# A planned TensorE order: two durations per operation, and stage times of their own for the first and last groups

## The chip, the cores and the metric

The kernel runs on one core of a Trainium2 chip. Five engines work side by side, each through its own list of instructions in a fixed order: PE (TensorE, matmuls and transposes; PEld is its weight load), DVE (VectorE), ACT (ScalarE), POOL (GpSimd) and SP (SyncE, which here only issues DMAs). An engine that reaches an instruction whose input is not there waits, and everything behind it on that engine waits too. The metric is the device time of one execution in microseconds; the kernel before has a median of 2764.06 us in 3 runs (2762.44 to 2764.56).

## The reference

Four graph layers on x (128 graphs, 128 nodes, 256 features) and adj (128 x 128 x 128, about 3% ones). Each layer is wrapped as `x = layernorm(x + layer(x, adj))`.

```python
# layer 0: attention by edge type (adj is 0 or 1 here)
e_k = leaky_relu(einsum('bid,bjd->bij', x * a_k, x)); alpha = where(adj == k+1, e_k, NEG_INF)
out = softmax(alpha) @ x
# layer 1: mean of messages
out = relu(x @ W_upd + (a.T @ (x @ W_msg)) / deg + bias)
# layer 2: three GRU steps
for i in range(3):
    aggr = einsum('bst,bsd->btd', A, h @ weight[i])
    gi, gh = aggr @ w_ih.T + b_ih, h @ w_hh.T + b_hh
    r, z = sigmoid(i_r + h_r), sigmoid(i_z + h_z); n = tanh(i_n + r * h_n)
    h = (1 - z) * n + z * h
# layer 3: additive attention
Wh = h @ W; e = leaky_relu(Wh @ a1 + (Wh @ a2).T); out = elu(softmax(where(adj > 0, e, NEG)) @ Wh)
```

## The kernel before

**Tiling.** The 128 graphs are taken in 32 groups of four (`G`, `NG`, lines 62 and 63). For each group the functions `loading`, `layer0`, `layer1`, `gru` (three times `step`) and `layer3` write down the group's operations; `weights` does so once for the weights. Nothing is issued at that time. A call such as `PE.matmul(...)` goes through `Engine.__getattr__` (line 188), which makes an `Op` with its engine, its operands, a planned duration and its dependences. This is why every instruction in the profile stands on one line, 232, the line of `issue`; groups of the profile are told apart by their tiles.

**The steps.** A GRU step works on features by nodes: `hT` holds two tiles of 128 features x 512 (four graphs of 128 nodes). `aggregate` multiplies the hidden state, split in three bf16 parts (`split`), by the adjacency matrix (`a_ne`) into `agT`. `gate` computes two 128 x 512 outputs of a gate with seven products instead of eight: products 1, 6, 7 and 4 are added one after another into one PSUM bank (`shared`), and after each of them ScalarE copies the bank's first half (`snapshot`, line 717) before the next may be added; products 2, 5 and 3 go into another bank. A step has gates q (hidden part of the candidate), t_r and t_z, two direct products (`direct`), and at the end `update`, which makes the new `hT` on VectorE. VectorE then transposes it in 32 x 32 blocks (`turned`), and two DMAs through DRAM (`way_h` out, `hn` back) finish the transpose; `split` makes the parts for the next aggregation. The `sums` that products 5, 6, 7 and 4 need are made on GpSimd from `hT` (`t_h`) and on VectorE from `agT` (`t_m`).

**The planner.** From line 921 a list scheduler puts the operations in order. It keeps for every engine a time at which it is free and a list of operations whose dependences are planned. It takes the engine that can start something first, and among that engine's operations that could start by then the one with the earliest due time (`nominal`; off TensorE an operation of a GRU step counts as due `EAGER` us earlier, and a snapshot `RUSH` us earlier). The chosen operation is issued, so the order of this loop is the order of the instructions on each engine. The planned times themselves are not in the program: the chip's engines start when their semaphores allow.

Three things set the plan. First, the durations (lines 239 to 256): one figure per operation, for which the engine is held and after which the result can be used, and then a hop: `HOP` to a step's operation, `PE_HOP` to one on TensorE, `SLACK` to any other; a DMA lands `LANDING` after its issue. Second, the due times: `paced(start, end)` spreads the operations recorded since the last call over a stretch, in units of `PERIOD` (82.744 us), the same for each group but for its number:

```python
    PERIOD = 82.744
    EAGER, RUSH = 5.34, 0.516
    L0_START, L0_END, L1_START, L1_END, L3_START, L3_END = -2.032, -1.293, -0.75, -0.05, 0.173, 0.919
```

So group g's layer 0 is due from g - 2.032 to g - 1.293 periods, its steps from g on, its layer 3 after step 2; several groups are under way at a time, and while one group's step waits for VectorE or a DMA, TensorE is given another's layer. Third, the buffers: a tile can be taken when the planner sees its last use done. VectorE and GpSimd share a port: an operation that `holds` it delays one that `waits` for it (lines 205 to 211 and 951).

The last group's layer 3 is written in two halves of two graphs, and the first group's and the last group's transposes go through TensorE (`turned_quick`, `end`) where the others go through DMAs.

Of the kernel before, what the change touches and what calls it, by code (L numbers as in the profile page):

```python
# [18 lines left out]
def kernel(  # L19
# [40 lines left out]
    P = 128  # L60
# [81 lines left out]

    FAST = ("tensor_scalar", "tensor_scalar_add", "tensor_scalar_mul")

    def m_of(view):
# [9 lines left out]
    class Op:  # L155
        def __init__(self, engine):
            self.engine, self.calls, self.took, self.landing = engine, [], 0.0, 0.0
            self.after, self.bufs, self.waiting = {}, [], 0
            self.ready, self.nominal, self.urgent = 0.0, 0.0, False
            self.waits = self.holds = False  # L160
            self.rush = 0.0

    class Engine:
# [24 lines left out]
        def __getattr__(self, name):  # L188
            def call(*args, **kw):
# [7 lines left out]
                ins = [v for v in (*rest, *named.values()) if isinstance(v, View)]  # L197
                n = 1
                for v in out + ins:
                    n = max(n, m_of(v))  # L200
                short = self is PE and BF16 in [v.buf.dtype for v in ins]
                op.took += SPLIT if short else self.cost(name, n, "accum_out" in kw)
                op.landing = LANDING if name == "dma_start" else 0.0

                tensors = [v for v in ins if m_of(v) > 4]
                if self is POOL:
                    op.waits, op.holds = True, name == "memset" or len(tensors) > 1
                elif self is DVE and name not in ("transpose", "bn_stats"):
                    op.waits = op.holds = not any(v.buf.pool is psum for v in out + tensors) and (
                        len(tensors) > 1 or (name in FAST and m_of(out[0]) > 4)  # L210
                    )
# [26 lines left out]

    LANDING = 4.2
    HOP = 0.235  # L240
    PE_HOP = 0.55
    SLACK = 0.873

    def pe_cost(op, n, sums):
        return 0.11 if op == "transpose" else 0.222 if n <= P else 0.003 + n / 599.0

    SPLIT = 0.056

    def dve_cost(op, n, sums):
        return 0.14 + n * (0.00056 if op in FAST else 0.00106)  # L250

    def act_cost(op, n, sums):
        return 0.6 if op == "dma_start" else 0.17 + n * 0.001 + (0.2 if sums else 0.0)

    def pool_cost(op, n, sums):
        return 0.2 + n * 0.00266 if op in FAST else 0.55 if op == "memset" else 1.2 if n < 64 else 0.25 + n * 0.0023

# [3 lines left out]
    POOL = Engine("POOL", nc.gpsimd, pool_cost)  # L261
    SP = Engine("SP", nc.sync, lambda op, n, sums: 0.6)
    engines = (PE, DVE, ACT, POOL, SP)


    PERIOD = 82.744
    SPAN = 2.0
    EAGER, RUSH = 5.34, 0.516
    L0_START, L0_END, L1_START, L1_END, L3_START, L3_END = -2.032, -1.293, -0.75, -0.05, 0.173, 0.919
    H_END, M_START, M_END = 0.179, 0.179, 0.503  # L270

    def paced(start, end, pe_only=False):

        took = [op.took if not pe_only or op.engine is PE else 0.0 for op in line]
        total, sofar = sum(took), 0.0
        for op, t in zip(line, took):
            op.nominal = (start + (end - start) * sofar / total) * PERIOD
            op.urgent = pe_only
            sofar += t
        line.clear()  # L280

    def row(v, n):
# [25 lines left out]
    def weights():  # L308
# [3 lines left out]
        for src, tag, bufs in ((w_ih, "hT", 6), (w_hh, "rest", 4)):  # L312
# [4 lines left out]
            if src is w_ih:  # L317
                for i in range(NL):
                    w = tile_of("hn", [P, KC, D], 3)
                    ACT.dma_start(out=w, in_=weight[i].rearrange("(c p) e -> p c e", p=P))  # L320
                    wnat.append(w)
        paced(-2.6, -2.5)
        for k, a in enumerate((a0, a1, a2, a3)):
            SP.dma_start(out=acol[:, k, :], in_=a.rearrange("(c p) -> p c", p=P))
        paced(-2.2, -2.1)
        SP.dma_start(out=w_um[:, :, :D], in_=w_upd.rearrange("(c p) u -> p c u", p=P))
# [6 lines left out]
        SP.dma_start(out=arow, in_=row(a_att, 2 * D))  # L333
        paced(-2.0, -1.5)

# [81 lines left out]
        for c in range(KC):  # L417
            DVE.tensor_sub(w3x[:, c, :], w3x[:, c, :], ps[:, : 2 + D])
        paced(-1.9, -0.2)

# [87 lines left out]
    def loading(g, s):  # L508
        graphs = slice(g * G, (g + 1) * G)
        s.x_blocks = tile_of("x_blocks", [P, KC, 4 * G, 32])  # L510
        s.adj = tile_of("adj_in", [P, G, N], 1, I32)
        s.x = tile_of("x_in", [P, G, D])
        for c in range(KC):
            for j in range(4):
                f0 = c * P + j * 32
                SP.dma_start(
                    out=s.x_blocks[j * 32 : (j + 1) * 32, c],
                    in_=x[graphs, :, f0 : f0 + 32].rearrange("b (i r) f -> r (b i) f", r=32),
                )
        SP.dma_start(out=s.adj, in_=adj[graphs].rearrange("b i j -> i b j"))  # L520
        paced(g - 2.4, g - 2.1)
        SP.dma_start(out=s.x, in_=x[graphs].rearrange("b n d -> n b d"))
        paced(g - 1.9, g - 1.8)

# [118 lines left out]
    def gru(g, s):  # L643
# [5 lines left out]
        def step(i, hT, parts):  # L649
# [53 lines left out]
            def gate(tag, q, sources, copied, added, last=None):  # L703
# [14 lines left out]
                def snapshot(quarter):  # L718
                    copied(t[:, quarter], shared[:, :H], quarter // 2)
                    ops[-1].rush = RUSH  # L720

# [59 lines left out]

            at = g + i * SPAN / NL
            w_i = c_gi[:, i]
            of_h = sums(POOL, hT, w_hhT, w_sh, hT, "t_h")
            q0, q1 = gate("q", C, (of_h,), hidden, half_more)
            paced(at, at + H_END, True)
            aggregate(0)
            aggregate(1)
            paced(at + M_START - 0.03, at + M_START, True)
            of_m = sums(DVE, agT, w_i, w_sm[:, i], agps, "t_m")  # L790
# [5 lines left out]
            update(0, z0, n0, d0)  # L796
            paced(at + M_START, at + M_END, True)
            return new, turning, split_up
# [104 lines left out]
    for g in range(NG):  # L903
        s = State()
        loading(g, s)
        layer0(g, s)
        paced(g + L0_START, g + L0_END)
        layer1(g, s)
        paced(g + L1_START, g + L1_END)
        gru(g, s)  # L910
        if g < NG - 1:
            layer3(g, s, 0, G)
            paced(g + SPAN + L3_START, g + SPAN + L3_END)
        else:

            for b in range(0, G, 2):
                layer3(g, s, b, b + 2)
                paced(g + SPAN + L3_START, g + SPAN + L3_END)

# [28 lines left out]
    def start_of(op):  # L948

        at = op.ready  # L950
        if op.waits:
            at = max(at, (POOL if op.engine is DVE else DVE).held)
# [18 lines left out]
    while left:  # L971
        best = None
        for e in engines:
# [5 lines left out]
            if best is None or at < best[0]:  # L979
                op = min(  # L980
                    (op for t, op in starts if t <= at),
                    key=lambda op: op.nominal - (EAGER if op.urgent and e is not PE else 0.0) - op.rush,
                )
# [7 lines left out]
        e.ready.remove(op)  # L991
        e.free = at + op.took
        if op.holds:
            e.held = e.free - 0.14
        end = e.free + op.landing
        for buf in op.bufs:
            buf.left -= 1
            buf.free_at = max(buf.free_at, end)
        for other in op.after.values():
            other.waiting -= 1  # L1000
            hop = 0.0 if other.engine is e and not op.landing else SLACK if not other.urgent else HOP
            if hop == HOP and other.engine is PE:
                hop = PE_HOP
            other.ready = max(other.ready, end + hop)
            if other.waiting == 0:
# [30 lines left out]
```

## Time and profile before

| what | us |
| --- | --- |
| median of 3 runs | 2764.06 (2762.44 to 2764.56) |
| profiled execution, first to last instruction | 2761.8 |
| PE busy | 2702.3 (98%) |
| DVE busy | 2304.1 (83%) |
| POOL, ACT busy | 1666.2 (60%), 1584.2 (57%) |
| DMA engines | 117 GB/s on average |
| mean granted TensorE clock | 0.991 |

The profiled execution's own time beside its span is not given separately: its span of 2761.8 us lies 2.3 us under the median. "Busy" of PE needs care: a matmul's record lasts 0.16 us beyond the moment at which the next may start, so an idle time under 0.16 us is not seen as idle, and a shown one is 0.16 short. The clock is the share of full speed that was granted to TensorE. In the timeline, records of one kind that follow each other are merged ("x2"), and the bracket tells idle time and who ended it. An fp32 matmul makes two records.

### The profile page before, as it was taken

The numbers are of one execution on the slowest core, as the hardware profiler recorded it, in microseconds if no ns is written. First come the engines' busy times: TensorE is split into PE (matmuls) and PEld (weight loads), VectorE is DVE, ScalarE is ACT, GpSimd is POOL, SyncE is SP. The second block draws the span as 40 slices with busy tenths as digits, with TensorE's granted clock in tenths as the row PEclk, the third lists the DMA queues.
The fourth block names the chain that finished last, engine by engine and source line by source line (L and its number), as shares of the span: only waits on it lengthen the run. The fifth ranks groups of instructions, "written<-read, shape, count | busy, mean of one in ns | idle before, by whom it ended". The sixth has DMA issues, their size and how long they took to land.

```text
span 2761.8 us, 44048 instructions
## 1 busy us (share of the span) xinstructions
PE 2702.3 (98%) x13756; PEld 2138.1 (77%) x13756; DVE 2304.1 (83%) x5108; ACT 1584.2 (57%) x3704; POOL 1666.2 (60%) x1606
## 2 busy tenths in 40 slices
PE   8899999999999999999999999999999999999996
PEld 5677787887887887887887887887887887787774
DVE  5787888888888888888888888888888898888875
ACT  4454665555665655665655665655665655665554
POOL 4544666655666655666655666655676655675542
PEclk9999999999999999999999999999999999999996
DMA  5545555555555556555655556655556555545441
GB/s 121 129 90 99 115 126 129 120 109 124 122 125 131 121 108 129 118 124 133 121 107 127 121 121 134 121 110 123 121 121 134 124 109 120 116 110 118 99 88 43
DMA packets 1397130, 321.88 MB, mean 117 GB/s; under 512 B 1142560, under 2 KB 1388448, under 8 KB 1396896
## 3 DMA queue, kind: packets, MB, share of 16 engines
q1 hardware_dynamic: 1394448, 316.69, 53.7%
q10 hardware_dynamic: 2448, 2.36, 0.3%
q8 instruction: 111, 1.82, 0.3%
q14 instruction: 123, 1.01, 0.1%
HBM read 185.74 MB, written 133.15 MB: 115 GB/s over the span
## 4 chain that ended last, share of the span: by engine, by line
PE 94%; DVE 3%; POOL 1%; ACT 1%; DMA 1%; issue 1%; ACTq 0%; POOLq 0%; DVEq 0%; SPq 0%
PE gate L232 52%; PE ps L232 42%; DVE t_r L232 0%; POOL t_h L232 0%; DVE xb L232 0%; DVE st L232 0%; DMA rest<-in_L_gnn_w_hh_dram 0%; DVE z L232 0%; POOL rstd L232 0%; DMA hn<-in_L_gnn_weight_dram 0%; POOL xa L232 0%; DVE xa L232 0%; DVE t_d L232 0%; POOL t_d L232 0%; DVE hT L232 0%
## 5 line engine op out<-in xcount | busy, mean ns | idle before, releaser
L232 ACT ACTIVATE q<-gate,bhn 128x256 f32<-128x256 f32 x384 | 183.0, 477 | 314.4 <-PE gate L232 313.1
L232 PE MATMUL ps<-agT,c_gi 128*128 128x512 f32 x768 | 356.0, 592 | 0.0
L232 PE MATMUL gate<-t_h,w_hhT 128*128 128x256 f32 x1152 | 345.2, 381 | 5.7 <-ACT t_z L232 4.3
L232 PE MATMUL gate<-t_h,w_sh 128*128 128x256 f32 x1152 | 337.1, 383 | 4.2 <-ACT q L232 1.7
L232 POOL TENSOR_TENSOR rstd<-rstd,neg_half 128x4 f32<-128x4 f32 (+1 forms) x128 | 142.4, 1112 | 218.2 <-DVE rstd L232 215.1
L232 PEld LDWEIGHTS gate<-t_h,w_sh 128*128 128x128 f32 x1152 | 213.7, 191 | 62.8 <-issue 30.4
L232 PEld LDWEIGHTS ps<-xs,xT 128*128 128x128 f32 x2048 | 249.7, 193 | 11.5 <-ACT xs L232 2.6
L232 PEld LDWEIGHTS gate<-t_h,w_hhT 128*128 128x128 f32 x1152 | 211.7, 191 | 56.1 <-issue 16.3
L232 PE MATMUL ps<-xs,xT 128*128 128x128 f32 x2048 | 251.8, 276 | 2.2 <-ACT xs L232 1.3
L232 ACT COPY t_z<-gate 128x256 f32<-128x256 f32 x288 | 107.1, 372 | 244.6 <-PE gate L232 244.0
L232 PE MATMUL ps<-w_um,x1T 128*128 128x512 f32 x512 | 237.1, 595 | 0.2 <-ACT x1T L232 0.2
L232 PEld LDWEIGHTS ps<-agT,c_gi 128*128 128x128 f32 x768 | 145.8, 190 | 114.5 <-issue 106.0
L232 PE MATMUL gate<-agT,c_gi 128*128 128x256 f32 x768 | 229.2, 380 | 2.6 <-ACT agT L232 2.6
L232 PE MATMUL gate<-t_m,c_gi 128*128 128x256 f32 x768 | 228.5, 379 | 0.0
L232 PE MATMUL gate<-t_m,w_sm 128*128 128x256 f32 x768 | 228.4, 379 | 0.0
L232 PE MATMUL gate<-hT,w_hhT 128*128 128x256 f32 x768 | 222.8, 385 | 5.6 <-DVE hT L232 5.6
L232 POOL TENSOR_SCALAR mk<-a_f 128x512 uint8<-128x512 f32 x128 | 201.3, 1579 | 12.2 <-DVE alpha L232 6.6
L232 ACT ACTIVATE xs<-xT,acol 128x512 f32<-128x512 f32 x256 | 182.1, 717 | 40.9 <-PE ps L232 31.5
L232 POOL MEMSET hu<- 128x1 f32 x128 | 10.3, 96 | 303.8 <-DVE fac L232 224.5
L232 DVE TENSOR_TENSOR t_z<-gate,t_z 128x256 f32<-128x256 f32 x192 | 104.2, 543 | 101.4 <-ACT t_z L232 53.7
L232 POOL TENSOR_TENSOR t_d<-h0T,t_n 128x512 f32<-128x512 f32 x64 | 82.9, 1295 | 174.0 <-ACT t_n L232 171.1
L232 PEld LDWEIGHTS gate<-hT,w_hhT 128*128 128x128 f32 x768 | 141.8, 191 | 48.1 <-issue 23.6
(197 smaller groups left out, 7280.1 us busy)
## 6 DMA issues: line engine op xcount, KB each, us to landing
way_h<-z SPq DMA_DIRECT2D x190, 256.0 KB, 2.4
hn<-way_h SPq DMA_DIRECT2D x760, 64.0 KB, 2.4
way<-z SPq DMA_DIRECT2D x126, 256.0 KB, 3.2
x_blocks<-in_x_dram SPq DMA_DIRECT2D x256, 64.0 KB, 2.3
x_in<-in_x_dram SPq DMA_DIRECT2D x32, 512.0 KB, 3.8
way_x<-xb SPq DMA_DIRECT2D x32, 512.0 KB, 2.9
way_p<-z SPq DMA_DIRECT2D x62, 256.0 KB, 2.6
probT<-way_p SPq DMA_DIRECT2D x248, 64.0 KB, 2.3
```

What stands on the lines that cost most here:

```text
L232: getattr(self.engine, name)(*[a.real() if isinstance(a, View) else a for a in args], **{k: a.real() if isinstance(a, View) else a for k, ...
```

## The change

The planner's model and its due times are replaced; the operations, their dependences and the buffers stay as they are.

- An operation has two durations: `took`, for which its engine is held, and `lasts`, after which its result can be used. Each engine's cost function returns both and sees the operands: operands in PSUM, pointers (small per-partition operands), type.
- DMA landing times are given by tile (`LANDING`), 2.4 us where none is named, plus `DMA_SLACK` for what follows.
- The hops are 0.1223 us (`HOP`), 0.0904 (`PE_HOP`, to TensorE) and 0.3008 (`SLACK`); none from TensorE to TensorE.
- An operation of GpSimd or VectorE minds the shared port only if it holds the port itself; `waits` is gone.
- `PERIOD` is 82.17434. Due times are in us, by stage (`TIMES`; each GRU step has its own), with an offset per stage for each of the first six groups (`HEAD`) and the last six (`TAIL`). `RUSH` becomes a factor.

```diff
-    LANDING = 4.2
-    HOP = 0.235
-    PE_HOP = 0.55
-    SLACK = 0.873
-
-    def pe_cost(op, n, sums):
-        return 0.11 if op == "transpose" else 0.222 if n <= P else 0.003 + n / 599.0
...
-    def dve_cost(op, n, sums):
-        return 0.14 + n * (0.00056 if op in FAST else 0.00106)
-
-    def act_cost(op, n, sums):
-        return 0.6 if op == "dma_start" else 0.17 + n * 0.001 + (0.2 if sums else 0.0)
...
+    LANDING = {"e": 5.66, "adj_in": 4.0, "x_in": 3.85, "x1T": 3.53, "way_1": 3.2, "way_2": 3.0, "xc": 3.6, "way_f": 2.0}
...
+    def pe_cost(op, n, out, ins, pointers, sums):
+        split = any(v.buf.dtype == BF16 or v.steps[-2:-1] == (("bitcast", (BF16,), {}),) for v in ins)
+        took = 0.11 if op == "transpose" else 0.056 if split else 0.005 + m_of(out[0]) / 600.0
+        return took, took + 0.165
+
+    def dve_cost(op, n, out, ins, pointers, sums):
...
+        elif op in FAST + ("tensor_copy", "memset") and not in_psum(out + ins):
+            lasts = 0.145 + n * 0.00055
+        else:
+            lasts = 0.145 + n * 0.00106 + (0.07 if pointers else 0.0)
+        return lasts - 0.08 + (0.05 if sums else 0.0), lasts + (0.1 if sums else 0.0)
+
+    def act_cost(op, n, out, ins, pointers, sums):
+        if op == "dma_start":
+            return 0.6, 5.0
+        lasts = 0.162 + n * 0.00083 + 0.1 * pointers
+        return lasts - 0.104 + (0.12 if sums else 0.0), lasts + (0.11 if sums else 0.0)
...
+    def sp_cost(op, n, out, ins, pointers, sums):
+        return 0.55, LANDING.get(tag_of(out[0]) if out else "out", 2.4)
...
-    PERIOD = 82.744
-    SPAN = 2.0
-    EAGER, RUSH = 5.34, 0.516
-    L0_START, L0_END, L1_START, L1_END, L3_START, L3_END = -2.032, -1.293, -0.75, -0.05, 0.173, 0.919
-    H_END, M_START, M_END = 0.179, 0.179, 0.503
+    PERIOD = 82.17434
+    EAGER, RUSH = 6.3715, 0.5988
+    HOP, PE_HOP, SLACK, DMA_SLACK = 0.1223, 0.0904, 0.3008, 1.3968
+    STAGES = ("loading", "layer0", "layer1", "step0", "step1", "step2", "layer3")
+    TIMES = {
+        "loading": ((-192.0355, -194.8256), (-195.1940, -218.9603),),
+        "layer0": ((-184.2411, -119.2739),),
...
+    HEAD = (
+        (15.258, -41.724, -22.713, -15.756, -24.319, -11.692, -19.589),
...
+    TAIL = (
+        (9.621, -0.848, 16.081, -0.054, 9.477, -4.187, 4.687),
...
+    def paced(stage, part, g):
+
+        start, end = TIMES[stage][part]
+        at = g * PERIOD
+        if g < len(HEAD):
+            at += HEAD[g][STAGES.index(stage)]
+        elif g >= NG - len(TAIL):
+            at += TAIL[g - NG][STAGES.index(stage)]
+        spread(at + start, at + end, stage[:4] == "step")
...
     def start_of(op):
 
         at = op.ready
-        if op.waits:
+        if op.holds:
             at = max(at, (POOL if op.engine is DVE else DVE).held)
...
         e.free = at + op.took
+        end = at + op.lasts + (DMA_SLACK if op.dma else 0.0)
         if op.holds:
-            e.held = e.free - 0.14
-        end = e.free + op.landing
+            e.held = at + op.lasts - 0.12
...
-            hop = 0.0 if other.engine is e and not op.landing else SLACK if not other.urgent else HOP
-            if hop == HOP and other.engine is PE:
-                hop = PE_HOP
-            other.ready = max(other.ready, end + hop)
+            to_pe = other.engine is PE
+            if e is PE and to_pe:
+                ready = e.free
+            elif e is other.engine and not op.dma:
+                ready = end
+            else:
+                ready = end + (SLACK if not other.urgent else PE_HOP if to_pe else HOP)
+            other.ready = max(other.ready, ready)
```

Since the loading stage's second time lies before its first and each stretch runs from its later to its earlier end, a group's load of x_in is now due ahead of its x_blocks, and the blocks are due in reverse order.

## The prediction

> **What bounds the kernel now.** I read the busy times first, then one table of stages, then TensorE's waits and its timeline where the table shows idle time.
>
> ```profile
> span 2761.8 us, 44048 instructions
> PE 2702.3 (98%) x13756; PEld 2138.1 (77%) x13756; DVE 2304.1 (83%) x5108; ACT 1584.2 (57%) x3704; POOL 1666.2 (60%) x1606
> ```
>
> The table: stage, its length, busy us of PE, PEld, DVE, ACT, POOL, then granted clock.
>
> ```profile
> 0.00:83.00 83.00, 67.54 (x362) 49.90 (x362) 51.63 (x130) 35.78 (x77) 43.59 (x54) 0.98 0.58 128
> 83.00:165.00 82.00, 76.84 (x368) 57.86 (x369) 53.48 (x118) 38.36 (x88) 33.33 (x36) 0.98 0.51 104
> 1000.00:1083.00 83.00, 83.00 (x428) 66.19 (x427) 71.60 (x159) 49.08 (x116) 52.73 (x51) 1.00 0.58 122
> 2482.00:2565.00 83.00, 80.63 (x376) 62.15 (x375) 69.41 (x151) 43.57 (x101) 46.45 (x45) 0.98 0.51 107
> 2648.00:2731.00 83.00, 70.90 (x300) 52.03 (x299) 53.12 (x108) 38.34 (x93) 27.37 (x27) 0.90 0.31 67
> 2731.00:2762.00 31.00, 11.13 (x31) 6.62 (x29) 15.18 (x49) 16.94 (x44) 8.35 (x9) 0.59 0.13 43
> ```
>
> TensorE is the bound, and in the interior it is full. The chain of waits there repeats one piece every 82.67 us:
>
> ```profile
> 1010.79 3.44 PE ps L232 x12
> 1093.46 3.44 PE ps L232 x12
> ```
>
> From one matmul's start to the next the trace has medians of 0.216 us (256 columns), 0.429 (512), 0.112 (128 fp32), 0.218 (258), 0.056 (bf16). One group's matmuls at these come to 82.40, so a period loses 0.27 us, in pieces under 0.06. All 13756 records come to 2661 us; the span has 100 more: 36 before 331 us, 7 in the interior, 57 after 2480. The change can gain only at the two ends.
>
> Timeline of TensorE at three idle places (start, length, what, idle time before it and who ended it):
>
> ```profile
> 109.11 0.60 PE L232 MATMUL ps<-hu,a_f 128*128 128x257 f32 x2
> 112.11 1.22 PE L232 MATMUL gate<-hT,w_hhT 128*128 128x256 f32 x2 [2.40 <-DVE hT L232]
> 113.12 2.94 PE L232 MATMUL ps<-x_in,probT 128*128 128x256 f32 x8
> 115.89 0.59 PE L232 MATMUL gate<-t_h,w_hhT 128*128 128x256 f32 x2
> ...
> 2516.80 0.70 PE L232 MATMUL gate<-agT,c_gi 128*128 128x256 f32 x2 [1.72 <-ACT agT L232]
> ...
> 2717.61 0.59 PE L232 MATMUL gate<-t_m,w_sm 128*128 128x256 f32 x2
> 2718.67 0.70 PE L232 MATMUL gate<-t_h,w_sh 128*128 128x256 f32 x2 [0.46 <-ACT t_z L232]
> 2719.21 0.59 PE L232 MATMUL gate<-t_m,w_sm 128*128 128x256 f32 x2
> 2724.76 0.63 PE L232 MATMUL ps<-ident,hT 128*128 128x128 f32 x4 [1.86 <-DVE hT L232]
> ```
>
> An idle time is dearer than it looks. The pair at 2717.61 would hand over after 0.43; the next starts after 1.06 and its pair takes 0.54: 0.46 idle costs 0.73. After 2.40 idle the next ten records run at half speed (eight take 2.77 instead of 1.73).
>
> The rule for this is in the Trainium skill, "TensorE: Matmul & The Clock Gate", section on the HAM clock gate: the clock halves after an idle window of about 3.4 us. The rows show it halved after 2.40 already (granted clock 0.60 from 112 to 116); by the page's figure that stall would be worth 2.6 rather than 4.2, and the head's sum below 1.6 less.
>
> **The change, part by part.** No instruction is added or removed; the planner puts the same 15746 operations in another order. I built both and compared orders.
>
> *Durations.* The planner's figures now are the rows: the copy 128x256 that takes 0.372 was planned as 0.426 plus 0.55 before TensorE may use it, now as 0.374 plus 0.09. In itself this costs nothing on the chip; it shows in the order.
>
> *Close pairs.* A matmul into the shared bank must wait until ScalarE has copied the bank: 0.16 (drain) + 0.04 + 0.37 + 0.05 = 0.62 us of TensorE work must stand between. Pairs closer than 0.62 number 25 in the old order and 18 in the new. In the steps of groups 0 and 1: 5 against 0. From group 28 on: 15 against 11.
>
> *Head.* (a) Between steps 0 and 1 of group 0 the old order puts layer 1 of group 1 ahead of the last z products on TensorE and VectorE; new, the update of hT comes first and layer 1 fills the wait: 4.7 us of matmuls between the last z product and the matmul that waits, where the trace needs 3.9 (108.24 to 112.11). The stall at 112.11 goes: 2.56 + 0.58 + 1.04 = 4.2. (b) Then q, rest and agT waits up to 128 us, 3.8 by the same reckoning; two of the close pairs go and rest is split earlier: 2.5. (c) Two z pairs (168, 280 us): 1.5; one agT (79 us): 0.5. Sum 8.7; ends 4 and 10.
>
> *Start.* x_in and adj of group 0 now stand ahead of all x_blocks in SP's queue, 768 KB more; at the 217 to 339 GB/s of those first 12 us this is 2.3 to 3.5 us later x_blocks, and the first scores stand behind 5.7 us of weight matmuls instead of 10.8. TensorE waits there, and the moved weight matmuls fill the softmax wait of 2.0 at 38 us. GpSimd's masks, which waited 13.8 us for adj, come sooner; TensorE did not wait for them. I take +0.6, ends -2 and +4.
>
> *Tail.* The agT stall at 2516.80 (1.88, then slowed records 1.5: 3.4), one q stall (1.0) and one z pair each in steps 2 of groups 30 and 31 (1.5) go; one z pair comes (-0.7). Two matmul pairs of group 30's layer 3 move from ahead of group 31's last z products to behind them: its hT comes 1.7 sooner. Sum 6.9; ends 3 and 8.
>
> *End.* Group 30's two output pairs (1.73) move ahead of the transposes that wait 1.86 for hT: -1.7. The transposes of wh for the last two graphs move from behind the other half's output, at 2744.57, to just behind its alpha transposes, at 2741.08 to 2741.7; the last chain hangs on them: -2.7. Together 4.4; ends 1 and 7 (the 2.66 wait at 2735 too).
>
> *Interior.* The order now has period two, with one 0.86 spacing (0.24 over the need) in odd groups and four or five in even ones; the old one has one per group, which cost nothing visible. A copy kept waiting behind one ScalarE activation of 0.72 would lose 0.48: 1.7 more such spacings a group, 28 groups, at most 23 us; at best all 7 lost now come back. I take +2: nearest to the row that shows no cost.
>
> *The other queues.* VectorE (83%), ScalarE and GpSimd carry the same work with slack; if VectorE came late by an instruction (0.69), the matmul behind it would. GpSimd's one-tensor operations no longer wait in the plan for VectorE's held port; no row prices that alone, it lies in the interior's ends.
>
> *Sum.* Gains 8.7 + 6.9 + 4.4 = 20.0. Where a stall goes, the next dependence is nearer; I let a quarter return: +5. With +0.6 and +2, 2761.8 - 12.4 = 2749.4. The median of the runs stands 2.3 above the profiled execution: 2752.
>
> **The rivals.** Measured against no change, 0.2% is 5.5 us.
>
> *Slower: the interior stalls.* Plans with 0.1 us of margin meet real jitter every period, with no idle time to absorb it. For it: TensorE at 83.00 of 83. Against: the new figures equal the rows. At the bound, 23 instead of 2: 2773. It beats the gains from 0.5 us per period.
>
> *Gains return.* Group 31's own chain (steps, then layer 3) sets the end whatever comes before, and the start's loads cost 4: only a third of 20 is left, 2752 + 9 = 2761. For it: 31 us with 11 of matmul at the end.
>
> *More.* No return, the loads hidden: 2761.8 - 20 - 2 + 2.3 = 2742.
>
> *No change at all* is excluded: the orders differ on every engine.
>
> **How the numbers follow.** Forecast 0.62, interior 0.16, return 0.14, more 0.08. The forecast's own range is 2744 to 2758. The range from 2740 to 2768 leaves out the dear end of the interior case and little below. Faster: nearly all of forecast and more, 0.68; same: most of return and the cheap part of interior, 0.16; slower: 0.16.
>
> **What would show it.** In the trace after: no wait for hT over 1 us near 110; no z wait at 168 and 280; PE busy over 80 of the second stage's 82; interior period 82.67 or less over two groups; the last alpha wait under 3.9. The prediction is wrong if the interior's period is 83.2 or more, if TensorE waits for x_blocks beyond 4 us, or if the last stage keeps its 31 us.

## The result and the profile after

The changed kernel takes 2783.71 us (median of 4 runs, 2780.87 to 2784.09), the kernel before 2764.31 in the same comparison: a ratio of 1.0068, with a 95% interval of 1.0055 to 1.0080. It is slower by 19 us where 12 us of gain were forecast, and outside the range.

The page of the changed kernel's profiled execution (span, then busy time and share of each engine):

```profile
span 2782.2 us, 43897 instructions
PE 2714.9 (98%) x13756; PEld 2129.4 (77%) x13756; DVE 2239.4 (80%) x5108; ACT 1581.6 (57%) x3704; POOL 1672.0 (60%) x1606
```

The same operations run, and VectorE is even busy for less time (2239.4 us, 2304.1 before). TensorE's records number the same, so the 20.4 us of longer span are time in which TensorE does not run at its own spacing. The stages, as the prediction showed them (stage, length, busy us of PE, PEld, DVE, ACT, POOL, clock, DMA share, GB/s):

```profile
0.00:83.00 83.00, 69.83 (x375) 52.07 (x376) 49.22 (x132) 36.58 (x79) 43.19 (x53) 1.00 0.52 128
83.00:165.00 82.00, 79.31 (x382) 61.42 (x381) 56.55 (x124) 38.64 (x87) 38.78 (x42) 0.96 0.48 99
1000.00:1083.00 83.00, 81.16 (x418) 64.11 (x418) 68.67 (x153) 47.89 (x113) 52.18 (x51) 1.00 0.57 119
2482.00:2565.00 83.00, 81.49 (x411) 63.79 (x410) 64.28 (x149) 44.08 (x103) 48.70 (x50) 1.00 0.52 106
2648.00:2731.00 83.00, 76.24 (x367) 58.03 (x365) 61.55 (x120) 43.83 (x101) 40.26 (x37) 0.95 0.44 92
2731.00:2782.00 51.00, 31.36 (x120) 21.57 (x117) 29.16 (x81) 28.30 (x74) 12.65 (x12) 0.77 0.14 37
```

The two head stages are fuller by 2.3 and 2.5 us. The stage in the interior, where TensorE was busy for 83.00 of 83, is down to 81.16 (418 records instead of 428). From here on I use one measure, the *loss*: the length of a stretch less all TensorE records that start in it, each at the median spacing that the prediction gives for its form. Both kernels have 2661.2 us of such work.

| loss, us | to 331 us (head) | 331 to 2480 (interior) | from 2480 (tail) |
|---|---|---|---|
| before | 36.1 | 7.0 | 57.5 |
| after | 29.2 | 47.2 | 44.6 |
| difference | -6.9 | +40.2 | -12.9 |

The sum is +20.4, the difference of the spans. The two ends together gained what was forecast; the interior lost twice that. TensorE's waits in the interior (who waits, for what: us in total, times, longest). The kernel after:

```profile
PE gate L228 <- POOL t_h L228: 6.8, 20, 1.6
PE gate L228 <- ACT t_z L228: 5.1, 9, 0.6
PE gate L228 <- DVE q L228: 4.9, 8, 0.7
PE gate L228 <- ACT t_r L228: 2.8, 6, 0.8
PE ps L228 <- DMA x1T<-way: 1.1, 2, 0.7
PE gate L228 <- DVE t_r L228: 0.2, 1, 0.2
```

The kernel before has the heading of this view and nothing under it:

```profile
core 0 of [0], span 2761.8 us
engine line waited for: us in total, times, longest us
```

Three engines are late in turn, none of them always. Two of these waits, followed back in the timeline of the kernel after. First one for t_h:

```profile
1254.11 0.73 POOL L228 TENSOR_TENSOR t_h<-hT 128x256 f32<-128x256 f32 x1
...
1254.68 0.71 DVE L228 SCALAR_TENSOR_TENSOR t_d<-t_z,t_d 128x512 f32<-128x512 f32 x1
...
1254.83 2.70 POOL L228 TENSOR_SCALAR xa<-xa,mv,rstd 128x256 f32<-128x256 f32 x1
1255.31 0.68 DVE L228 SCALAR_TENSOR_TENSOR xb<-xb,xa 128x512 f32<-128x512 f32 x1
1255.92 0.68 DVE L228 SCALAR_TENSOR_TENSOR hT<-t_d,t_n 128x512 f32<-128x512 f32 x1
...
1257.49 0.73 POOL L228 TENSOR_TENSOR t_h<-hT 128x256 f32<-128x256 f32 x1
...
1258.96 0.70 PE L228 MATMUL gate<-t_h,w_sh 128*128 128x256 f32 x2 [0.17 <-POOL t_h L228]
```

GpSimd's xa took 2.70 us; alone it takes 1.22. It started 0.15 us after VectorE's first two-tensor instruction, and two more followed without a gap, until 1256.60: xa got on only then. The t_h behind it came 1.5 us late; the matmul that needs it started 0.33 us late, so the rest of the delay was room. Now one in which VectorE waits for GpSimd:

```profile
1278.34 0.74 DVE L228 TENSOR_TENSOR rest<-rest 128x512 bf16<-128x512 f32 x1
...
1278.54 1.63 POOL L228 TENSOR_TENSOR t_d<-hT,t_n 128x512 f32<-128x512 f32 x1 [0.31 <-ACT t_n L228]
...
1278.97 1.22 DVE L228 SCALAR_TENSOR_TENSOR nmr<-mv,rstd 128x4 f32<-128x4 f32 x1
...
1280.22 1.09 ACT L228 ACTIVATE xb<-xb,nmr,rstd 128x256 f32<-128x256 f32 x2 [1.51 <-DVE nmr L228]
...
1281.84 0.35 ACT L228 COPY t_z<-gate 128x256 f32<-128x256 f32 x1
...
1282.23 0.70 PE L228 MATMUL gate<-t_h,w_hhT 128*128 128x256 f32 x2 [0.62 <-ACT t_z L228]
```

nmr has 4 elements a partition and takes 0.15 us alone; here it stood 1.22 us behind GpSimd's two-tensor t_d, which itself had stood behind VectorE's rest. ScalarE's two xb waited 1.51 us for nmr, the copy of t_z stood behind them and xs in ScalarE's queue, and TensorE lost 0.78 us (0.62 shown as idle, and the 0.16 by which a shown idle time is short). The same wait of TensorE comes at 1113.17 and 1452.04: 169.1 and 169.8 us apart, two groups of 84.5 to 84.9 us instead of 82.67.

The Trainium skill, "SBUF — State Buffer", section "Who interferes with whom", has the rule: VectorE and GpSimd share one pair of ports, a VectorE instruction with two SBUF inputs contends with a GpSimd instruction that reads SBUF, and the one that comes second stands still until the first is through. The rows agree for xa and nmr.

A piece of loss is the delay of one TensorE record behind its median spacing. In the whole interior 59 pieces exceed 0.15 us, 31.8 us in sum. Followed back as above over at most 6 us, some 43 of them (22 us) have an instruction on their path that was stretched by at least 60% of what was lost. Some of these can stand there by chance: the same count in e13 below, with as many stretched instructions a group, gives 15 of 59 (4.6 of 42.9 us). The kernel before has no piece over 0.06.

Yet collisions are no novelty. Counting VectorE's and GpSimd's instructions that lasted over 0.1 us more than the shortest twentieth of their kind, the kernel before has 20.0 a group, 9.2 us of stretch, and the kernel after 20.5 and 9.4. One kind in the view of groups (count, busy us, mean ns, idle before), before and then after:

```profile
L232 POOL TENSOR_SCALAR xb<-xb,mv,rstd 128x256 f32<-128x256 f32 x62 | 108.6, 1757 | 3.2
...
L232 POOL TENSOR_SCALAR xa<-xa,mv,rstd 128x256 f32<-128x256 f32 x62 | 87.9, 1420 | 3.4
```

```profile
L228 POOL TENSOR_SCALAR xa<-xa,mv,rstd 128x256 f32<-128x256 f32 x62 | 95.9, 1549 | 3.1
...
L228 POOL TENSOR_SCALAR xb<-xb,mv,rstd 128x256 f32<-128x256 f32 x62 | 78.2, 1265 | 2.3
```

Before, one of a group's two xb took some 2.47 us in nearly every group of the interior (mean 1757), and TensorE lost nothing by it; after, xb is almost free of it (1265), xa is worse, and TensorE waits. So the question for the runs was which part of the change turned harmless collisions into harmful ones.

### The profile page after: what moved, and what is told of

Read it like the earlier page. It is cut to its first block, busy times and chain, and to the rows that moved or that the text cites. A ratio compares the mean times of both kernels' runs of the same rounds, so it can differ in the third digit from the quotient of the medians.

```text
span 2782.2 us, 43897 instructions
## 1 busy us (share of the span) xinstructions
PE 2714.9 (98%) x13756; PEld 2129.4 (77%) x13756; DVE 2239.4 (80%) x5108; ACT 1581.6 (57%) x3704; POOL 1672.0 (60%) x1606
## 4 chain that ended last, share of the span: by engine, by line
PE 71%; DVE 16%; POOL 5%; ACT 3%; DMA 3%; issue 2%; SPq 1%; DVEq 0%; POOLq 0%; ACTq 0%
PE gate L228 39%; PE ps L228 31%; DVE rest L228 2%; DVE t_r L228 2%; DVE st L228 1%; DVE t_m L228 1%; DVE t_d L228 1%; POOL xa L228 1%; DVE hT L228 1%; POOL t_h L228 1%; DVE z L228 1%; SPq L228 1%; DVE xb L228 1%; POOL rstd L228 1%; POOL xb L228 1%
## 5 line engine op out<-in xcount | busy, mean ns | idle before, releaser
L228 PE MATMUL gate<-t_h,w_sh 128*128 128x256 f32 x1152 | 344.3, 385 | 9.9 <-POOL t_h L228 4.3
L228 PEld LDWEIGHTS gate<-t_h,w_sh 128*128 128x128 f32 x1152 | 207.7, 190 | 62.6 <-POOL t_h L228 15.0
L228 POOL TENSOR_TENSOR rstd<-rstd,neg_half 128x4 f32<-128x4 f32 (+1 forms) x128 | 149.3, 1166 | 163.1 <-DVE rstd L228 144.6
L228 POOL TENSOR_TENSOR t_d<-hT,t_n 128x512 f32<-128x512 f32 x128 | 177.7, 1393 | 99.5 <-ACT t_n L228 99.1
L228 POOL TENSOR_TENSOR t_d<-h0T,t_n 128x512 f32<-128x512 f32 x64 | 90.4, 1412 | 235.1 <-ACT t_n L228 235.1
L228 POOL TENSOR_SCALAR mk<-a_f 128x512 uint8<-128x512 f32 x128 | 209.6, 1643 | 22.6 <-DVE alpha L228 14.1
L228 ACT ACTIVATE t_r<-t_r,brz 128x256 f32<-128x256 f32 x192 | 117.9, 614 | 161.8 <-DVE t_r L228 150.0
L228 ACT COPY t_r<-gate 128x256 f32<-128x256 f32 x288 | 107.2, 372 | 145.5 <-PE gate L228 144.4
```

What stands on the lines that cost most here:

```text
L228: getattr(self.engine, name)(*[a.real() if isinstance(a, View) else a for a in args], **{k: a.real() if isinstance(a, View) else a for k, ...
```

## The experiments

All figures of loss are head / interior / tail, in us, as in the table above (after: 29.2 / 47.2 / 44.6); the 47.5 in the expectations is the same interior, cut a little later. Ratios are against the kernel before.

**e1, the three old margins.** The stalls look like thin margins; this puts the wide ones back.

```diff
-    HOP, PE_HOP, SLACK, DMA_SLACK = 0.1223, 0.0904, 0.3008, 1.3968
+    HOP, PE_HOP, SLACK, DMA_SLACK = 0.235, 0.55, 0.873, 1.3968
```

> The changed kernel with the three margins of the kernel before (HOP 0.235, PE_HOP 0.55, SLACK 0.873); durations, stage times, HEAD and TAIL as changed. In its order the round trips TensorE to another engine to TensorE that have under 0.3 us to spare fall from 3.7 a period to 0.7 (1.0 in the kernel before). Theory M (thin margins): the loss of TensorE from 331 to 2480 us, 47.5 us in the changed kernel and 6.9 before, falls under 15, and the time under 2765; the head and tail gains of 20 may shrink, since they were planned with the small margins. Theory W (GpSimd and VectorE planned onto their shared port at once) and theory P (a PERIOD without room): the loss stays at 35 to 50, the time at 2775 to 2790. Theory C (any reshuffle moves the time by this much): anything between 2745 and 2800.

2819.73 us, ratio 1.0201 (1.0184 to 1.0218); loss 33.3 / 61.3 / 61.7. Theory M's forecast fails: with 0.7 thin round trips a period instead of 3.7 the interior is worse, not better. (The run mixes wide margins with stage times that were set for narrow ones; e13 comes back to this.) The first wait of its interior:

```profile
PE gate L228 <- POOL t_h L228: 23.5, 33, 2.1
```

What is late most is GpSimd's t_h, by up to 2.1 us, beyond any margin of this size. The tail went back to 61.7, so the tail's gain does not outlast the small margins.

**e2, the port waits back.** In the kernel before, every GpSimd operation waits in the plan for VectorE's held port; in the change only those that hold it themselves.

```diff
-            self.holds = False
+            self.waits = self.holds = False
...
-                    op.holds = name == "memset" or len(tensors) > 1
+                    op.waits, op.holds = True, name == "memset" or len(tensors) > 1
...
-                    op.holds = not any(v.buf.pool is psum for v in out + tensors) and (
+                    op.waits = op.holds = not any(v.buf.pool is psum for v in out + tensors) and (
...
-        if op.holds:
+        if op.waits:
             at = max(at, (POOL if op.engine is DVE else DVE).held)
```

> The changed kernel in which GpSimd's one-tensor operations wait again in the plan for VectorE's held port, as in the kernel before. Theory W: the loss from 331 to 2480 us falls under 20, and the time to 2745 to 2758. Theories M and P: it stays at 35 to 55 (round trips with under 0.3 us to spare are 4.0 a period, not fewer), time 2775 to 2790.

2763.35 us, ratio 0.9997 (0.9988 to 1.0006); loss 28.7 / 25.0 / 46.5. The interior recovers 22 of its 40 us. Theory W has the direction, but both its figures (a loss under 20, 2758 us at most) are missed; the ends stay within 2 us. TensorE's waits in the interior are now

```profile
PE gate L228 <- ACT t_z L228: 3.1, 6, 0.9
PE gate L228 <- DVE q L228: 2.2, 3, 1.2
PE ps L228 <- DVE xd L228: 1.6, 1, 1.6
PE ps L228 <- PE gate L228: 0.4, 1, 0.4
```

and t_h is gone from them. Of the 25.0 us only 10.0 are left in pieces over 0.15 us (16 of them), and 5 of these (2.9 us) have a stretched instruction on their path. Collisions as a whole did not become fewer: 28.0 a group with 12.7 us of stretch, against 20.5 and 9.4. But those of GpSimd's one-tensor instructions, which the dropped rule is about, did: 1.3 us of stretch a group against 2.0. So the run does not tell whether the plan now foresees these collisions or avoids them.

**e3, the old PERIOD.**

```diff
-    PERIOD = 82.17434
+    PERIOD = 82.744
```

> The changed kernel with PERIOD 82.744 instead of 82.174, the value before; all else as changed. Theory P: the loss from 331 to 2480 us falls under 20, time 2745 to 2758. Theories M and W: it stays at 35 to 55 (3.4 thin round trips a period), time 2775 to 2790; a list order does not hold work back for a later date.

2774.99 us, ratio 1.0036 (1.0023 to 1.0049); loss 31.1 / 31.5 / 49.3. Between the theories: 16 us of the interior come back, neither under 20 nor over 35.

**e4, a change without meaning.**

```diff
-    EAGER, RUSH = 6.3715, 0.5988
+    EAGER, RUSH = 6.45, 0.5988
```

> The changed kernel with EAGER 6.45 instead of 6.3715, a change without meaning that only reshuffles the order. Theories M, W and P: the loss stays within 10 us of 47.5 and the time within 8 of 2784. Theory C (the time hangs on the accident of the order): a difference of more than 10 us either way.

2778.15 us, ratio 1.0049 (1.0034 to 1.0064); loss 29.2 / 41.5 / 45.7. A mere reshuffle is worth 6 us in the interior. Smaller effects of a parameter cannot be told from it, and e3's not by much.

**e5, the kernel before without the port waits.**

```diff
-                    op.waits, op.holds = True, name == "memset" or len(tensors) > 1
+                    op.waits = op.holds = name == "memset" or len(tensors) > 1
```

> The kernel before with one part of the change alone: GpSimd's one-tensor operations no longer wait in the plan for VectorE's held port. Theory W (the dropped port wait makes collisions that the plan does not see, and t_h comes late from GpSimd): the loss of TensorE from 331 to 2480 us rises from 7 to 20 to 35, with waits for t_h, time 2778 to 2795. Theory T (the tables of the first and last six groups and the new stage times do it; the waits only matter with them): the loss stays under 14, time 2758 to 2771.

2763.57 us, ratio 0.9997 (0.9987 to 1.0006); loss 35.2 / 11.8 / 53.5. Alone the dropped waits cost the interior 5 us, which the ends gave back. Theory W as I had put it ("20 to 35") is wrong for this order; the figures are those of theory T.

**e6, port waits back and no tables.** The lines of e2, and

```diff
     HEAD = (
-        (15.258, -41.724, -22.713, -15.756, -24.319, -11.692, -19.589),
...
+        (0,) * 7,
...
     TAIL = (
-        (9.621, -0.848, 16.081, -0.054, 9.477, -4.187, 4.687),
...
+        (0,) * 7,
...
```

> The changed kernel with the port waits restored and HEAD and TAIL set to zero; the new durations, margins, PERIOD and TIMES stay. Theories W and T together (the waits cost 22, the tables' offsets, which pull the groups out of one rhythm, most of the other 18): the loss from 331 to 2480 us falls to 5 to 12; the head loses the table's gain (29 back to 30 to 37), the tail keeps the margins' gain (44 to 50): time 2744 to 2757. If thin margins in themselves cost the other 18, the loss stays at 20 to 27 and the time at 2762 to 2772.

2763.37 us, ratio 0.9996 (0.9986 to 1.0006); loss 41.1 / 14.4 / 42.8. The interior is nearly calm (just over the 12 expected) and its waits amount to

```profile
PE ps L228 <- DMA x1T<-way: 0.4, 1, 0.4
PE ps L228 <- PE gate L228: 0.2, 1, 0.2
```

although collisions are at their highest, 30.8 a group with 14.1 us of stretch. Without HEAD the head is worse than in the kernel before, 41.1 where I expected 30 to 37, and that keeps the time above the 2757 expected; without TAIL the tail is as good as ever.

**e7, no tables, waits dropped as in the change.** The tables' edit of e6 alone.

```diff
     HEAD = (
-        (15.258, -41.724, -22.713, -15.756, -24.319, -11.692, -19.589),
...
+        (0,) * 7,
...
     TAIL = (
-        (9.621, -0.848, 16.081, -0.054, 9.477, -4.187, 4.687),
...
+        (0,) * 7,
...
```

> The changed kernel with HEAD and TAIL set to zero, port waits dropped as in the change. Theory W: the collisions are still unplanned, loss from 331 to 2480 us 25 to 40, time 2766 to 2782. Theory T: the loss falls under 15, time 2745 to 2760.

2799.48 us, ratio 1.0126 (1.0111 to 1.0141); loss 43.5 / 44.6 / 49.3. The interior stays bad without the tables, so they are not its cause (theory T falls); it is also worse than theory W's 25 to 40, and the time is above all expectations because the head is lost as well. The waits make 30 us between e7 and e6.

**e8, GpSimd's normalisation shortened.** The changed order, but GpSimd's share of xa, xb, xc and xd works on 32 of its 256 columns.

```diff
             for name, args, kw in op.calls:
+                if self is POOL and name in FAST and len(args) > 1 and args[0].buf is args[1].buf:
+                    args = (args[0][:, :32], args[1][:, :32], *args[2:])
                 getattr(self.engine, name)(
```

> The changed kernel's order to the last instruction, but GpSimd's normalisation (xa, xb, xc, xd; eight a group, 1.2 us each and up to 2.7 where they collide) works on 32 of its 256 columns; the other columns stay unnormalised. Theory W (these are what collides and what t_h stands behind on GpSimd): the waits for t_h (6.8 us) go, the loss from 331 to 2480 us falls from 47 to under 25, time under 2762. If the loss comes from hops or durations planned too short on ScalarE and VectorE, it stays over 38 and the time over 2774.

2785.79 us, ratio 1.0078 (1.0063 to 1.0093); loss 27.7 / 50.4 / 42.7. The wait for t_h goes as expected, the loss does not:

```profile
PE gate L230 <- DVE q L230: 14.3, 10, 1.9
...
PE gate L230 <- POOL t_h L230: 1.3, 2, 1.0
```

VectorE's q came late instead, and at least 28 of this kernel's 59 pieces over 0.15 us still have a stretched instruction on their path. So these operations alone are not the cause. My reading is that the shorter work moved GpSimd's other, two-tensor instructions onto VectorE's, and that moving one collision makes others; but the figures are also those that the expectation gave to the rival, hops or durations on ScalarE and VectorE planned too short (over 38, over 2774), and this run does not exclude it.

**e9, VectorE's small operations wait too.** As e6, and

```diff
+                    op.waits = op.waits or (name in FAST or len(ins) > 1) and not in_psum(out + ins)
```

> As e6 (port waits restored, HEAD and TAIL zero), and VectorE's small operations (rstd, nmr, ninv, 4 elements each), which neither kernel plans for the port, wait in the plan for GpSimd's lock as well. Theory U (what costs TensorE is not a collision but one that the plan has not foreseen): the instructions stretched by over 0.1 us stay near e6's 31 a period, or more than the 20 of the kernel before, and still the loss from 331 to 2480 us falls from e6's 14 to 10 or less; time 2755 to 2761. Rival (the 7 left over the kernel before come from the small margins): it stays at 12 to 17, time 2761 to 2767.

2767.87 us, ratio 1.0013 (1.0004 to 1.0022); loss 43.7 / 17.6 / 43.9. The small operations were stretched less often (1.4 a group, 3.9 in e6), but nothing was gained. Theory U, that foreseeing more collisions must calm the interior further, is not borne out for these.

**e10, e9 with HEAD.** The lines of e2 and e9, and of the tables only TAIL at zero.

```diff
     TAIL = (
-        (9.621, -0.848, 16.081, -0.054, 9.477, -4.187, 4.687),
...
+        (0.000, -0.000, 0.000, -0.000, 0.000, -0.000, 0.000),
...
```

> As e9, with the HEAD table of the change back (TAIL stays zero). Theories U and T: the head's loss returns to 28 to 30 (41 without the table), the tail keeps 42 to 44, the table's offsets cost the interior 5 to 11 over e9: time 2747 to 2757. Rival (the gains at the ends do not add up with a calm interior, because what is not lost in one place is lost in the next): time 2759 to 2766.

2753.94 us, ratio 0.9966 (0.9954 to 0.9978): faster than both kernels. Loss 26.8 / 17.8 / 45.3: the time is as the theories have it, the head gains more than expected, and HEAD's offsets cost the interior nothing over e9. The rival, that the gains do not add up, falls. Its page:

```profile
span 2751.1 us, 43992 instructions
...
PE 2705.5 (98%) x13756; PEld 2132.9 (78%) x13756; DVE 2301.1 (84%) x5108; ACT 1583.7 (58%) x3704; POOL 1688.0 (61%) x1606
```

VectorE is busy for 62 us more than in the slower changed kernel: its busy time holds the time by which its instructions are stretched, and this kernel, with more of it, is the faster one.

**e11, e10 with another PERIOD.**

```diff
-    PERIOD = 82.17434
-    EAGER, RUSH = 6.3715, 0.5988
+    PERIOD = 82.5
+    EAGER, RUSH = 6.3715, 0.516
```

> As e10, with PERIOD 82.5 (82.174) and RUSH 0.516 (0.5988). With HEAD, a PERIOD nearer to what a group really takes (82.67 in the kernel before) costs nothing in a plan whose collisions are foreseen, as it gave 16 us of the interior's loss in e3 where they were not: loss from 331 to 2480 us at or under e10's, time 2745 to 2755. If PERIOD helped in e3 by the accident of another order only: within 5 us of e10 either way.

2765.99 us, ratio 1.0003 (0.9994 to 1.0012); loss 29.0 / 30.6 / 43.8. Neither expectation holds: here a longer PERIOD (with another RUSH) costs 13 us of the interior where in e3 it gave 16. PERIOD has no direction of its own, and 13 us is what such a turn of two parameters can do by itself.

**e12, the durations and margins alone.** The changed kernel with the lines of e2, and pacing as in the kernel before.

```diff
-    PERIOD = 82.17434
-    EAGER, RUSH = 6.3715, 0.5988
+    PERIOD = 82.744
+    SPAN = 2.0
+    EAGER, RUSH = 5.34, 0.516
...
-            paced(f"step{i}", 0, g)
+            paced(at, at + H_END, True)
...
```

> The two durations and the new margins alone: stage times, PERIOD, EAGER and RUSH of the kernel before, port waits kept. Theory D (the durations and margins make the interior sensitive): its loss from 331 to 2480 us is over 15. Theory S (the stage times do): under 12, with the tail's gain in part, time 2745 to 2760. Theory J (stage times are set for one set of durations and are calm only with it): over 25, time over 2770, and e13 likewise.

2839.95 us, ratio 1.0273 (1.0257 to 1.0289); loss 41.1 / 79.7 / 56.5.

```profile
PE gate L228 <- ACT q L228: 13.8, 22, 0.7
```

The loss is far over theory S's 12; theories D and J both allow it. The largest wait in sum is now one for ScalarE's q.

**e13, the stage times alone.** The kernel before with the change's pacing.

```diff
-    PERIOD = 82.744
-    SPAN = 2.0
-    EAGER, RUSH = 5.34, 0.516
+    PERIOD = 82.17434
+    EAGER, RUSH = 6.3715, 0.5988
...
-            paced(at, at + H_END, True)
+            paced(f"step{i}", 0, g)
...
```

> The new stage times alone (PERIOD, EAGER, RUSH, TIMES, HEAD, TAIL), with the old single durations, margins and port waits. Theory D: loss from 331 to 2480 us under 12, time 2750 to 2765. Theory S: 15 to 40. Theory J: over 25, time over 2770.

2812.70 us, ratio 1.0177 (1.0163 to 1.0191); loss 34.4 / 54.2 / 61.7. Theory J: either half of the change alone is far worse than both kernels. That fits stage times that are set for one set of durations. Its losses are mostly of another kind: only 15 of its 59 pieces over 0.15 us have a stretched instruction on their path. This is also why e1, which mixed old margins with new stage times, could not tell whether margins are thin.

**e14, e10 without the small waits.** The lines of e2, and TAIL at zero; against e10:

```diff
-                    op.waits = op.waits or (name in FAST or len(ins) > 1) and not in_psum(out + ins)
```

> The changed kernel with the port waits restored and TAIL zero, HEAD as changed; the small operations wait for nothing in the plan. If HEAD with a zero TAIL makes e10 fast, this comes within 4 of e10's 2754; e9 against e6 (17.4 against 14.2 lost) says that the small waits gave nothing, so 2750 to 2757. If the small waits are what HEAD needs, 2758 to 2766.

2757.04 us, ratio 0.9975 (0.9965 to 0.9984); loss 29.6 / 21.5 / 44.2. HEAD with a zero TAIL and the old port waits carry e10; the 3 us between them are no more than a reshuffle.

**e15, e14 without the port waits.** Against the changed kernel, one edit:

```diff
     TAIL = (
-        (9.621, -0.848, 16.081, -0.054, 9.477, -4.187, 4.687),
...
+        (0.000, -0.000, 0.000, -0.000, 0.000, -0.000, 0.000),
...
```

> The changed kernel with TAIL zero, its port waits dropped as in the change: e14 without the waits. Theory W (the waits are worth 20 to 30 us in the interior whatever the rest): the loss from 331 to 2480 us is 40 to 52 where e14 has 21.7, time 2775 to 2788. Chance: within 12 us of e14 either way, so 10 to 34.

2782.73 us, ratio 1.0067 (1.0052 to 1.0082); loss 28.1 / 44.7 / 49.0. As theory W has it, and outside what chance was given. A third pair: the waits are worth 23 us of the interior.

**e16, e3 with the port waits.** The lines of e2, and

```diff
-    PERIOD = 82.17434
+    PERIOD = 82.744
```

> e3 (PERIOD 82.744) with the port waits restored. Theory W: the loss from 331 to 2480 us falls from e3's 31.7 to 5 to 18, time 2748 to 2762. Chance: within 12 us of e3 either way, so 20 to 44, time 2763 to 2787.

2763.19 us, ratio 0.9997 (0.9987 to 1.0006); loss 29.0 / 25.3 / 47.5. Only 6 us, within chance; theory W's 5 to 18 fails here. The five pairs in one table:

| interior's loss | waits dropped | waits kept | difference |
|---|---|---|---|
| change as it is (after, e2) | 47.2 | 25.0 | 22 |
| no tables (e7, e6) | 44.6 | 14.4 | 30 |
| TAIL zero (e15, e14) | 44.7 | 21.5 | 23 |
| PERIOD 82.744 (e3, e16) | 31.5 | 25.3 | 6 |
| the kernel before (e5, before) | 11.8 | 7.0 | 5 |

With the change's PERIOD the waits are worth 22 to 30 us three times out of three, more than the 6 and 13 that turns of other parameters moved. With 82.744 they are worth 5 or 6. Why the longer PERIOD bears the dropped waits isn't settled: no run separates it from the accident of the order.

Nor is it settled how the waits help. In the first three pairs the stretch of GpSimd's one-tensor instructions falls with them by 0.8, 1.1 and 0.9 us a group, or 20, 28 and 22 us over the 26 groups of the interior, close to the loss that goes; so they may help by avoiding these collisions rather than by foreseeing them. Against it, the fourth pair's falls by 1.3 us a group, 33 us, and only 6 us of loss go.

## Why the prediction was wrong

*Head, -8.7 and +0.6.* The sum is about right, -6.9 measured, but its parts are not, and that is luck. (a) The wait for hT near 110 us is gone, as TensorE's timeline after shows:

```profile
109.22 0.59 PE L228 MATMUL gate<-t_h,w_hhT 128*128 128x256 f32 x2
109.66 0.59 PE L228 MATMUL gate<-hT,w_sh 128*128 128x256 f32 x2
110.09 1.95 PE L228 MATMUL ps<-xs,xT 128*128 128x128 f32 x16
111.87 0.22 PE L228 MATMUL ps<-a_ne,hn 128*128 128x128 bf16 x1
113.24 0.23 PE L228 MATMUL ps<-a_ne,rest 128*128 128x128 bf16 x1 [1.15 <-DVE rest L228]
114.20 0.23 PE L228 MATMUL ps<-a_ne,rest 128*128 128x128 bf16 x1 [0.73 <-DVE rest L228]
```

Other matmuls run at 109 to 112; what is late next is rest, with 1.15, 0.73 and 0.48 us up to 116.24, and the granted clock is 0.57 from 114 to 122 us. So (a) and (b), 6.7 us of forecast gain between 83 and 165 us, brought 1.3 (loss 8.3 before, 7.0 after), and the second stage came to 79.31 busy us instead of the 80 I had named. (c) No z wait is left between 160 and 300 us; 165 to 331 us gained 2.9. The start was priced at +0.6 and gained: the first 83 us lost 24.2 before and 21.4 after, TensorE is busy for 2.3 us more in them and waits for x_blocks nowhere.

What I had not seen is where the gain comes from: HEAD. Without it the head loses 41.1 (e6) or 43.5 (e7), with it 29.6 (e14) or 28.1 (e15).

*Tail and end, -6.9 and -4.4.* Right: 11.3 forecast, 12.9 measured. The last wait for alpha is 1.40, under the 3.9 named; the longest of the end is now one for xT, 3.67 us, which was 2.23 before:

```profile
2750.25 0.66 PE L228 MATMUL ps<-ident,hT 128*128 128x128 f32 x4
...
2763.39 0.86 PE L228 MATMUL ps<-ident,xT 128*128 128x128 f32 x2 [3.67 <-ACT xT L228]
...
2769.18 0.77 PE L228 MATMUL ps<-ident,alpha 128*128 128x128 f32 x2 [1.40 <-ACT alpha L228]
```

From the first transposes of the last hT to the end it is 37.0 us before (from 2724.76 in the prediction's rows) and 32.0 after. The gain doesn't come from TAIL: with the waits, TAIL zero is 2.3 us better (e14 against e2), without them 4.4 worse (e15). It needs the new margins, durations and stage times together, as far as the runs go: the tail loses 56.5 to 61.7 where one of them is old (e1, e12, e13).

*A quarter of the gains returned, +5.* Not seen in the sum: 6.9 + 12.9 = 19.8, and 20.0 - 0.6 were forecast before the return. Between 83 and 165 us most of the gain did return (5.4 of 6.7); gains elsewhere that were not forecast made up for it.

*Interior, +2, ends -7 and +23.* Wrong, and this decides the result: +40.2. The prediction looked for new stalls in one place, the spacing of two uses of the shared bank around ScalarE's copy, and priced 1.7 of those a group. Such stalls exist (t_z and t_r in the view of waits), but in the one followed back above the copy is late because of what went before on VectorE. The step that failed is the one on the other queues: that GpSimd's one-tensor operations no longer wait in the plan for VectorE's port "lies in the interior's ends", as "no row prices that alone". A row did. In the profile before, one and the same operation on 128x256 had means of 1757 ns as xb and 1420 as xa; alone it takes 1.22 us. With one mk and the cast a_f that makes four stretched one-tensor instructions of GpSimd a group, 2.3 us, in that trace. Were the plan not to foresee them and TensorE to wait for each, 26 groups of the interior would pay 60 us: that is the end that the range lacked, and it holds the 40 measured. It is an upper end and no forecast: in the old order the same step cost 5 us (e5).

What the runs showed in its place: the port waits are worth 22 of the 40 us (e2), and two more pairs with the change's PERIOD have 30 and 23. The cause of the remaining 18 stays open. 10 of them are pieces over 0.15 us, most without a stretched instruction on their path, and 8 are smaller ones. With the tables at zero as well they are down to 7 (e6), but HEAD's offsets cost 7 us in one order (e14 against e6) and nothing in another (e10 against e9), and mere turns of a parameter moved 6 and 13. The half that keeps the old stage times (e12) and the half that keeps the old durations (e13) both lose more. That the new durations equal the rows, which the rival's case counted against itself, says nothing on it: they are the durations without a collision.

*The rival "the interior stalls"* had the right place, the right falsifier (a period of 83.2 or more; it is 84.5 to 84.9) and half the price, and it got a chance of 0.16. Its mechanism, 0.1 us of margin against jitter, wasn't shown: the stalls I followed back come from stretches of 0.3 to 1.5 us, and those that return do so nearly unchanged (nmr, ahead of the waits at 1113, 1282 and 1452 us, by 1.08, 1.07 and 1.07), which is no jitter, and wider margins without matching stage times made it worse (e1).

## What to carry to other kernels

When a planner drops a rule on a shared resource, look in the old profile for the same operation with different means: the excess per period, times the periods, is the upper end of the price if the plan no longer foresees it (here 60 us, of which one order paid 5 and another 22). Where the bound engine is full in every period, price an interior by that end rather than by the row that shows no cost, because one late result in 80 us is multiplied by the number of periods while the gains at the ends come once. Stage times and durations of such a planner are one set; each is tested with the other, and a meaningless turn of a parameter (here 6 us, and 13 for two parameters) tells how much of a result is accident.

## What the runs showed of the hardware

What the instruction in front is decides too, not only which comes first. The figures are medians over VectorE's two-tensor 128x512 instructions without PSUM that started while one of GpSimd had over 0.3 us to go. Behind a two-tensor instruction of GpSimd they took 0.91 us longer with 1.01 to go (108 cases of t_d in e6), and 0.45 longer with 0.55 to go (125 cases of t_h): all but the last 0.1 us. Behind a TENSOR_SCALAR of GpSimd they were hardly held up: by 0.18 us with 1.19 to go (89 cases of mk in the kernel after, 0.46 at most), and by 0.06 with 0.86 to go (37 cases of xb in e6). Having one tensor is not what matters: behind the cast a_f, which has one too, they took 0.31 us longer with 0.43 to go (26 cases in the kernel before). The other way round a TENSOR_SCALAR of GpSimd does stand, as xa did for 1.5 us. The section of the Trainium skill named above has the later instruction blocked in either order; for a TENSOR_SCALAR of GpSimd in front, these rows differ.

More collision went with less time: e6 and e10 have 14.1 and 12.8 us of stretch a group, the kernel after 9.4, and they are 20 and 30 us faster. So the sum of the stretch does not tell the price here; which instruction is stretched may, and what room the plan leaves behind it; no run separates the two.
